# A 3x3 convolution stage on one core: four combinations of kept rows moved behind the last step's first additions, and split by images in the last output half

## The chip, the cores and the metric

The kernel runs on one core of a Trainium2 chip. Its time is the device time of one execution in microseconds (us); lower is better. A core has TensorE (PE: matrix products into PSUM, an accumulator memory of eight banks), VectorE (DVE), ScalarE (ACT), GpSimd (POOL), and DMA queues that are fed from SyncE (SP) and from POOL. Each engine works through its own list of instructions in order; semaphores make one engine wait for another, and an instruction of an engine wait for an earlier one of its own.

## What is computed

For an input `x` of 8 images with 512 channels of 32x32 in float32:

```python
def _L0_conv_ref(x, ...):                 # C = 256, 4 heads of 64, N = 2
    t = cbs(x, cv1_w, cv1_bn, 0)          # cbs: convolution, batch norm, SiLU
    ys = [t[:, :C], t[:, C:]]
    for i in range(N):
        yi = ys[-1]
        z = cbs(yi, m_cv1_w[i], m_cv1_bn[i], 1)      # the 3x3 convolution
        z = bot_attention(z, m_qkv_w[i], m_rw[i], m_rh[i])
        z = silu(bn_eval(conv2d(z, m_cv2_w[i], 0), m_cv2_bn[i]))
        ys.append(yi + z)
    return cbs(concatenate(ys, axis=1), cv2_w, cv2_bn, 0)
x = x + _L0_conv_ref(_gn(x), ...)         # _gn: group norm, 32 groups
```

The change is inside the 3x3 convolution `z = cbs(yi, m_cv1_w[i], ...)`.

## The kernel before

**Passes.** The eight images go through in four passes of two (`p` = 0 to 3, `G = 2` images a pass). In each pass stand a first 3x3 convolution (`n = 0`), projections and attention of either image, a 1x1 convolution `m2`, then the same with a second 3x3 convolution (`n = 1`), then the output convolution `cv2`. The products of `cv1` for the next pass are laid between. So there are eight 3x3 convolutions, each for both images at once. Projections, `cv1` and `cv2` mostly use Strassen's seven products instead of eight.

**The 3x3 convolution** (`conv3x3`, L610). It uses a Winograd form for tiles of 4x4 outputs: the input rows and columns are transformed to six values each (`v_in`, made by DVE before), the weights too (`u`, loaded), PE multiplies, and DVE transforms back. For each of two output halves of 128 channels (`oc`) there are three steps `i`, one for each pair of the six row values; a step has 96 matrix instructions in the profile.

In a step PE first writes the products of four of the six column values into one PSUM tile (`inner_ps`), then those of the other two into a second one (`outer_ps`). Both come from the pool `ps_big`, which has room for three tiles in turn, so a tile is free again for PE once DVE has read the one that stood there three tiles earlier. Then:

- ACT copies one bank of the inner tile to SBUF (`c_m`, L658);
- DVE adds and subtracts the other bank and the copy (`c_t`, L672 and L673; the *additions* below). L673 is the last to read the inner tile. In the last step of the last output half (`parts = groups`) both are split into one for each image;
- L680 (`c_e`) brings in the outer tile, and is the last to read it; L687 to L690 make the two rows `r0`, `r1` (`c_r`);
- steps 0 and 1 keep their sum and difference (`c_k`, L693 and L694): `s_`, `d_` from step 0, `big_s`, `big_d` from step 1;
- at the end of step 1 come **the four combinations of kept rows** (L698 to L701): output rows 1 and 2 of each tile are written from the kept values, and `big_s`, `big_d` are overwritten by what rows 0 and 3 need;
- in step 2, the last one, L703 and L704 (first and last output row) finish `z`, and ACT applies batch norm and SiLU in place (L495), for each image and each half of its rows.

In step 1 of the last output half, POOL also forms the difference `t_z` (`first_sum`, L900) out of the already finished output half 0, for the projection behind (not in pass 0's first convolution).

**The projection behind** (`project_strassen`, L902) starts with image 0: first PE products of output half 0 (`to_qk`, L916), then `to_v` (L922) into a tile of `ps_big`, then L916 on output half 1, which needs the last SiLU of image 0. Pass 0's first convolution is followed by a plain projection (`project_direct`) instead. `q` stands in the SBUF place of the additions' results, and `kr` in that of the kept rows.

**What sets the order.** The Tile framework's scheduler orders every engine's list when the program is built; `with tc.issue_after(x)` forbids it to put what is inside ahead of `x`. ACT keeps one set of function tables; a change from SiLU to Exp or back costs an ACT_TABLE_LOAD.

Of the kernel before, what the change touches and what calls it, by code (L numbers as in the profile page):

```python
# [47 lines left out]
ALU = mybir.AluOpType  # L48
# [13 lines left out]
def kernel(  # L62
# [43 lines left out]
    stt, tt = nc.vector.scalar_tensor_tensor, nc.vector.tensor_tensor  # L106
# [384 lines left out]
    def stages(act, small, ps_big, ps_av, n_pt):  # L491
# [16 lines left out]
        def table_of(func):  # L508

            return nc.scalar.activation(spare, zero, func)  # L510
# [99 lines left out]
        def conv3x3(n, vs, u_of, z, groups=G, summed=None, after=None, between={}):  # L610

            q = TILES * groups
            work = act.tile([P, 2, 2, 4, q], F32, tag="q", name="c3_t")
            keep = act.tile([P, 2, 2, 4 * q], F32, tag="k", name="c3_k")
            turn, t = 0, None
            s_, d_, big_s, big_d = (keep[:, i, j] for i in range(2) for j in range(2))

            def tiles(ap):
                return ap.rearrange("p (t w) -> p t w", w=F)

            for oc in range(NM):
                dst = z[:, oc].rearrange("p g x -> p (g x)").rearrange("p (t r w) -> p r t w", r=4, w=F)
                for i in range(NI):
                    us = u_of(oc, i)
                    m = work[:, turn % 2]
                    turn += 1
                    e_t = act.tile([P, 4 * q], F32, tag="rs", name="c3_e", bufs=4)
                    inner_ps, outer_ps = (
                        ps_big.tile([P, 2, HALF], F32, tag="big", name="c3_ps") for _ in range(2)
                    )  # L630

                    def slots(ps, bank):
                        return ps[:, bank, : 4 * q].rearrange("p (r a q) -> p r a q", r=2, a=2)

                    places = {
                        1: (inner_ps, 0, 0), 2: (inner_ps, 1, 0), 3: (inner_ps, 0, 1), 4: (inner_ps, 1, 1),
                        0: (outer_ps, 0, 0), 5: (outer_ps, 0, 1),
                    }
                    for cps in ((1, 2), (0,)):
                        if (turn, cps[0]) in between:  # L640
                            between[turn, cps[0]](conv_product[0])
                        for row in range(2):
                            for cp in cps:
                                for c in range(2):
                                    ps, bank, at = places[CPS[cp][c]]
                                    to = slots(ps, bank)[:, row, at]
                                    for k in range(NM):
                                        rhs = vs[i, cp][:, c].rearrange(
                                            "p g (r t k s) -> p g r t k s", r=2, t=NT, k=NM
                                        )[:, :, row, :, k]  # L650
                                        for h in range(2):
                                            o = slice(h * HD, (h + 1) * HD)
                                            conv_product[0] = nc.tensor.matmul(  # L653
                                                to[o], us[cp][:, k, row, c, o], rhs,
                                                start=(k == 0), stop=(k == NM - 1),
                                            )
                    m24 = act.tile([P, 2, 2, q], F32, tag="h", name="c3_m", bufs=2)
                    copied = nc.scalar.copy(m24, slots(inner_ps, 1))  # L658
                    if after:
                        with tc.issue_after(copied.ins):  # L660
                            after()
                        after = None
                    r_t = act.tile([P, 8 * q], F32, tag="acc", name="c3_r", bufs=2)
                    final = i == NI - 1
                    parts = groups if final and oc == NM - 1 else 1
                    n_q = q // parts
                    by_part = {"g": parts, "r": 2, "q": n_q}
                    m_t = m.rearrange("p r a q -> p (r a q)")
                    m_parts = m_t.rearrange("p (g r a q) -> p g r a q", a=4, **by_part)
                    for part in range(parts):  # L670
                        qs, m = ts(part, n_q), m_parts[:, part]
                        tt(m[:, :, 0::2], slots(inner_ps, 0)[..., qs], m24[..., qs], ALU.add)  # L672
                        tt(m[:, :, 1::2], slots(inner_ps, 0)[..., qs], m24[..., qs], ALU.subtract)  # L673
                    for part in range(parts):
                        qs, tl, xs_ = ts(part, n_q), ts(part, n_q // NT), ts(part, 4 * n_q)
                        m = m_parts[:, part]
                        e = e_t.rearrange("p (g r a q) -> p g r a q", a=2, **by_part)[:, part]
                        r = r_t.rearrange("p (g r t x s) -> p g r t x s", g=parts, r=2, x=4, s=NT)[:, part]
                        outer = slots(outer_ps, 0).rearrange("p r a q -> p (r a) q")[..., qs]
                        stt(e.rearrange("p r a q -> p (r a) q"), outer, -6.0, m[:, :, 0:2], ALU.mult, ALU.add)  # L680

                        def by_tiles(ap):
                            return ap.rearrange("p r (t s) -> p r t s", s=NT)

                        m0, m1, m2, m3 = (by_tiles(m[:, :, a]) for a in range(4))
                        e0, e1 = (by_tiles(e[:, :, a]) for a in range(2))
                        stt(r[:, :, :, 3], m2, -0.25, e0, ALU.mult, ALU.add)  # L687
                        stt(r[:, :, :, 2], m3, -0.5, m1, ALU.mult, ALU.add)
                        tt(r[:, :, :, 1], m0, m2, ALU.subtract)
                        stt(r[:, :, :, 0], m3, -2.0, e1, ALU.mult, ALU.add)  # L690
                        r0, r1 = (r[:, j].rearrange("p t x s -> p (t x s)") for j in range(2))
                        if i < 2:
                            tt(keep[:, i, 0], r0, r1, ALU.add)  # L693
                            tt(keep[:, i, 1], r0, r1, ALU.subtract)  # L694
                        if i == 1:
                            if oc == NM - 1 and summed is not None:
                                t = first_sum(summed, nc.gpsimd)
                            stt(dst[:, 1], tiles(big_d), -0.5, tiles(d_), ALU.mult, ALU.add)  # L698
                            tt(dst[:, 2], tiles(s_), tiles(big_s), ALU.subtract)
                            stt(big_s, big_s, -0.25, s_, ALU.mult, ALU.add)  # L700
                            stt(big_d, big_d, -2.0, d_, ALU.mult, ALU.add)  # L701
                        if final:
                            stt(dst[:, 0, tl], tiles(r0), -6.0, tiles(big_s[:, xs_]), ALU.mult, ALU.add)  # L703
                            stt(dst[:, 3, tl], tiles(r1), -6.0, tiles(big_d[:, xs_]), ALU.mult, ALU.add)  # L704
                            per = groups // parts
                            for g in range(part * per, (part + 1) * per):
                                for half in range(NH):
                                    z_part = z[:, oc, g, ts(half, HALF)]
                                    last_silu = silu(z_part, z_part, bn_m1[n] + oc)
            if summed is None:  # L710
                with tc.issue_after(last_silu.ins):
                    table_of(AF.Exp)
            return t
# [183 lines left out]
        def first_sum(z, engine=nc.vector):  # L897

            t = act.tile([P, 2, HALF], F32, tag="pt", name="t_z", bufs=n_pt)
            engine.tensor_tensor(t[:, 0], z[:, 0, ts(1, HALF)], z[:, 0, ts(0, HALF)], ALU.subtract)  # L900
            return t
# [836 lines left out]
    with tc.issue_after(made.ins), tc.issue_after(s.silued[0].ins), tc.issue_after(first.ins):  # L1738
        multiplied, read, applied, powered = next(norm)
# [95 lines left out]
    for p in range(NP):  # L1835
# [5 lines left out]
        def u_of(n):  # L1841
            return lambda oc, i: [take(("u", n, oc, i, cp)) for cp in range(3)]
# [337 lines left out]
        if p == 0:  # L2180
            halves = load_halves()
            behind[1] = lambda: make_sw(halves)
            tiles = [act.tile([P, 3 * C], F32, tag=tag, name="qkv_raw") for tag in ("p3", "p4")]
# [198 lines left out]
```

## Time and profile before

| | before |
|---|---|
| median of 3 runs | 2251.07 us (2250.76 to 2251.08) |
| span of the profiled execution, first to last instruction | 2246.8 us |
| PE busy | 2200.9 us (98%) |
| DVE busy | 1728.7 us (77%) |
| ACT busy | 1099.6 us (49%) |
| POOL busy | 224.4 us (10%) |
| granted TensorE clock, mean | 0.999 |

The profile is one execution; its whole time is not given apart from the span, so the span is set beside the median of the runs, 4.27 us above it. Rows of a timeline give the start, the duration, the engine, the line, the operation, output<-inputs and their sizes, and in brackets the idle time of the engine just before and what ended it. The start is from the beginning of the span. An instruction's duration covers its whole way through the engine: the next one often starts before it has ended. Rows of the waits give total time, how often, and the longest. The chain of waits goes back from the last instruction, at each step to what released it.

### The profile page before, as it was taken

The numbers are of one execution on the slowest core, as the hardware profiler recorded it, in microseconds if no ns is written. First come the engines' busy times: TensorE is split into PE (matmuls) and PEld (weight loads), VectorE is DVE, ScalarE is ACT, GpSimd is POOL, SyncE is SP. The second block draws the span as 40 slices with busy tenths as digits, with TensorE's granted clock in tenths as the row PEclk, the third lists the DMA queues.
The fourth block names the chain that finished last, engine by engine and source line by source line (L and its number), as shares of the span: only waits on it lengthen the run. The fifth ranks groups of instructions, "written<-read, shape, count | busy, mean of one in ns | idle before, by whom it ended". The sixth has DMA issues, their size and how long they took to land.

```text
span 2246.8 us, 40264 instructions
## 1 busy us (share of the span) xinstructions
PE 2200.9 (98%) x16346; PEld 1080.6 (48%) x16346; DVE 1728.7 (77%) x2648; ACT 1099.6 (49%) x1332; POOL 224.4 (10%) x417
## 2 busy tenths in 40 slices
PE   7999999999999999999999999999999999999998
PEld 3653437343474444634447343654344734473443
DVE  7988879878678688877857868986794868797652
ACT  7554653644225665456324666455622455335533
POOL 4322210000220000000021000000012000000001
PEclk9999999999999999999999999999999999999999
DMA  9854447321581324511257141532136611350214
GB/s 273 308 163 150 150 151 261 109 78 45 140 275 49 118 81 145 183 58 67 67 159 261 30 169 35 197 116 77 58 76 173 233 39 34 102 198 30 67 50 112
DMA packets 134309, 285.60 MB, mean 127 GB/s; under 512 B 33540, under 2 KB 61184, under 8 KB 133092
## 3 DMA queue, kind: packets, MB, share of 16 engines
q1 hardware_dynamic: 102212, 197.34, 26.7%
q0 software_dynamic: 31904, 85.61, 13.3%
q8 instruction: 131, 2.15, 0.4%
q14 instruction: 62, 0.51, 0.1%
HBM read 214.86 MB, written 68.03 MB: 126 GB/s over the span
## 4 chain that ended last, share of the span: by engine, by line
PE 85%; DVE 11%; issue 1%; ACT 1%; DMA 1%; SPq 0%; POOL 0%; DVEq 0%; ACTq 0%; POOLq 0%
PE av_ps L1071 18%; PE l_ps L1037 18%; PE c L1305 9%; PE c_ps L653 7%; PE c_new L1305 6%; PE p_ps L916 6%; PE ps L523 5%; PE m_ps L1285 5%; PE x_ps L1405 4%; PE p_ps L922 3%; PE s_ps L1089 1%; DVE acc L1057 1%; DVE c_e L680 1%; PE p_ps L886 1%; DVE c_t L673 1%
## 5 line engine op out<-in xcount | busy, mean ns | idle before, releaser
L1041 ACT ACTIVATE pt<-l_ps 128x1024 f32<-128x1024 f32 x512 | 495.5, 1023 | 332.1 <-PE l_ps L1037 218.8
L1057 DVE TENSOR_TENSOR acc<-acc,pt 128x1024 f32<-128x1024 f32 x384 | 469.6, 1223 | 44.6 <-ACT pt L1041 16.2
L1071 PE MATMUL av_ps<-pt,vT 64*64 64x512 f32 x4096 | 484.8, 590 | 5.2 <-DVE z L1079 4.9
L1037 PE MATMUL l_ps<-q,kr 64*64 64x512 f32 x4096 | 486.3, 590 | 3.0 <-ACT pt L1041 1.9
L1071 PEld LDWEIGHTS av_ps<-pt,vT 64*64 64x64 f32 x4096 | 156.3, 133 | 284.8 <-issue 233.5
L1037 PEld LDWEIGHTS l_ps<-q,kr 64*64 64x64 f32 x4096 | 157.5, 133 | 273.2 <-issue 247.0
L653 PE MATMUL c_ps<-v_in,u 128*64 128x128 f32 x4320 | 239.1, 273 | 2.5 <-issue 2.5
L653 PEld LDWEIGHTS c_ps<-v_in,u 128*64 128x64 f32 x4320 | 235.8, 137 | 9.4 <-issue 9.4
L1285 PE MATMUL m_ps<-z,m_sb 128*128 128x512 f32 x256 | 114.1, 593 | 0.0
L658 ACT COPY c_m<-c_ps 128x512 f32<-128x512 f32 x48 | 28.0, 584 | 170.1 <-PE c_ps L653 140.8
L916 PE MATMUL p_ps<-t_z,sq 128*128 128x512 f32 x224 | 107.0, 595 | 0.0
L1079 DVE TENSOR_TENSOR z<-av_ps,z 128x512 f32<-128x512 f32 x64 | 44.1, 689 | 79.1 <-ACT z L1078 79.1
L1055 DVE TENSOR_TENSOR acc<-pt 128x1024 f32<-128x1024 f32 x64 | 78.0, 1219 | 18.0 <-PE s_ps L1089 11.2
L495 ACT ACTIVATE t<-m_ps,bh,sh 128x512 f32<-128x512 f32 x64 | 46.3, 773 | 91.2 <-PE m_ps L1285 91.2
L916 PE MATMUL p_ps<-z,sq 128*128 128x512 f32 x168 | 80.1, 604 | 5.3 <-ACT z L495 5.2
L1355 POOL DMA_DIRECT2D c_out<-in_x_dram x56 | 50.2, 954 | 293.2 <-ACT c_out L495 288.5
L1285 PEld LDWEIGHTS m_ps<-z,m_sb 128*128 128x128 f32 x256 | 47.8, 190 | 56.8 <-issue 52.5
L1147 DVE TENSOR_TENSOR z<-z,rs 128x512 f32<-128x512 f32 x64 | 42.3, 686 | 27.4 <-DMA rs<-r_dram 27.2
L495 ACT ACTIVATE c_out<-cz,bh,sh 128x512 f32<-128x512 f32 x14 | 16.8, 1301 | 89.1 <-DVE cz L1382 89.1
L495 ACT ACTIVATE z<-z,bh,sh 128x512 f32<-128x512 f32 x64 | 47.6, 804 | 25.8 <-DVE z L704 25.2
L1405 PE MATMUL x_ps<-t_x,sw 128*128 128x512 f32 x128 | 55.9, 592 | 0.0
L922 PEld LDWEIGHTS p_ps<-sq,z 128*128 128x128 f32 x336 | 42.7, 191 | 26.6 <-issue 12.7
(313 smaller groups left out, 3143.4 us busy)
## 6 DMA issues: line engine op xcount, KB each, us to landing
u<-u SPq DMA_DIRECT2D x135, 512.0 KB, 4.8
rs<-r_dram SPq DMA_DIRECT2D x126, 128.0 KB, 3.1
sq<-sq SPq DMA_DIRECT2D x42, 384.0 KB, 5.9
x<-in_x_dram SPq DMA_DIRECT2D x28, 512.0 KB, 7.0
r_in<-r SPq DMA_DIRECT2D x28, 512.0 KB, 4.9
y_in<-y SPq DMA_DIRECT2D x28, 512.0 KB, 4.4
c_out<-in_x_dram POOLq DMA_DIRECT2D x56, 256.0 KB, 5.1
out_dram<-c_out POOLq DMA_DIRECT2D x56, 256.0 KB, 3.3
```

Source lines behind the costliest of these rows:

```text
L495: silued[0] = nc.scalar.activation(dst, src, AF.Silu, scale=sh[:, k : k + 1], bias=bh[:, k : k + 1])
L523: last_product[0] = nc.tensor.matmul(ps[:, half, :], w_of(k), rhs_of(k, half), start=(k == begin), stop=(k == end))
L653: conv_product[0] = nc.tensor.matmul(to[o], us[cp][:, k, row, c, o], rhs, start=(k == 0), stop=(k == NM - 1),)
L916: nc.tensor.matmul(ps[:, o, :], w[:, o, :], rhs, start=not onto, stop=True, skip_group_check=onto)
L922: nc.tensor.matmul(v[:, ts(j, P)], rhs[:, ts(j, P)], w[:, 2, :], start=j == 0 and not onto, stop=True, skip_group_check=True,)
L1037: nc.tensor.matmul(ps[kh * HD : (kh + 1) * HD, hd, :], kr[r, c, o : o + HD], q[r, c, ts(half, HALF)], start=True, stop=True,)
L1041: last_exp[0] = exp = nc.scalar.activation(pt, ps, AF.Exp, scale=SCALE)
L1057: ins = nc.vector.tensor_tensor(accs[g], accs[g], pt[i], ALU.add)
L1071: nc.tensor.matmul(avs[g][hd * HD : (hd + 1) * HD, kh, :], vT[r, j, o : o + HD], pt[i][r, hd, :], start=(j == 0), stop=(j == NJ - 1),)
L1285: nc.tensor.matmul(pss[half][:, oc, :], m2_sb[:, n, k, ts(oc, P)], ao[:, k, ts(half, HALF)], start=(k == 0), stop=(k == NM - 1),)
L1305: nc.tensor.matmul(ps[:, o, :], w[:, k, ts(o, P)], rhs[part][:, c], start=(k == 0 and not onto), stop=(k == KB - 1), skip_group_check=onto,)
L1405: nc.tensor.matmul(ps[:, o, :], w[:, c, ts(o, P)], rhs[c], start=(c == 0 and not onto), stop=(c == 1), skip_group_check=onto,)
```

## The change

In the last step (`final`) the additions now remember the last of them (`read`), and the four combinations are issued behind it, for each part of the step. In output half 0 there is one part, so the combinations keep their size and only move from the end of step 1 to behind the additions of step 2. In output half 1 there are two parts, one for each image, so each combination becomes two of half the size, and each image's four stand ahead of that image's L680.

```diff
                     for part in range(parts):
                         qs, m = ts(part, n_q), m_parts[:, part]
                         tt(m[:, :, 0::2], slots(inner_ps, 0)[..., qs], m24[..., qs], ALU.add)
-                        tt(m[:, :, 1::2], slots(inner_ps, 0)[..., qs], m24[..., qs], ALU.subtract)
+                        read = tt(m[:, :, 1::2], slots(inner_ps, 0)[..., qs], m24[..., qs], ALU.subtract)
                     for part in range(parts):
                         qs, tl, xs_ = ts(part, n_q), ts(part, n_q // NT), ts(part, 4 * n_q)
                         m = m_parts[:, part]
+                        if final:
+                            s_p, d_p, big_s_p, big_d_p = (a[:, xs_] for a in (s_, d_, big_s, big_d))
+                            with tc.issue_after(read.ins):
+                                stt(dst[:, 1, tl], tiles(big_d_p), -0.5, tiles(d_p), ALU.mult, ALU.add)
+                                tt(dst[:, 2, tl], tiles(s_p), tiles(big_s_p), ALU.subtract)
+                                stt(big_s_p, big_s_p, -0.25, s_p, ALU.mult, ALU.add)
+                                stt(big_d_p, big_d_p, -2.0, d_p, ALU.mult, ALU.add)
...
                         if i == 1:
                             if oc == NM - 1 and summed is not None:
                                 t = first_sum(summed, nc.gpsimd)
-                            stt(dst[:, 1], tiles(big_d), -0.5, tiles(d_), ALU.mult, ALU.add)
-                            tt(dst[:, 2], tiles(s_), tiles(big_s), ALU.subtract)
-                            stt(big_s, big_s, -0.25, s_, ALU.mult, ALU.add)
-                            stt(big_d, big_d, -2.0, d_, ALU.mult, ALU.add)
```

Lines behind the inserted seven move: what was L680 is now L687, L687 to L690 are L694 to L697, L693 and L694 are L700 and L701, and from L703 on every line is 3 higher. The combinations are now L680 to L683.

**DVE, the end of a convolution** (pass 0, second convolution, output half 1, from the kept sums of step 1 to the outputs of image 0). Before:

```order
L694 TENSOR_TENSOR c_k<-c_r 128x512
L699 TENSOR_TENSOR z<-c_k 128x16x32
L698 SCALAR_TENSOR_TENSOR z<-c_k 128x16x32
L700 SCALAR_TENSOR_TENSOR c_k<-c_k 128x512
L701 SCALAR_TENSOR_TENSOR c_k<-c_k 128x512
L672 TENSOR_TENSOR c_t<-c_ps,c_m 128x4x64
L673 TENSOR_TENSOR c_t<-c_ps,c_m 128x4x64
L672 TENSOR_TENSOR c_t<-c_ps,c_m 128x4x64
L673 TENSOR_TENSOR c_t<-c_ps,c_m 128x4x64
L680 SCALAR_TENSOR_TENSOR c_e<-c_ps,c_t 128x256
```

Now the same place:

```order
L701 TENSOR_TENSOR c_k<-c_r 128x512
L672 TENSOR_TENSOR c_t<-c_ps,c_m 128x4x64
L673 TENSOR_TENSOR c_t<-c_ps,c_m 128x4x64
L672 TENSOR_TENSOR c_t<-c_ps,c_m 128x4x64
L673 TENSOR_TENSOR c_t<-c_ps,c_m 128x4x64
L680 SCALAR_TENSOR_TENSOR z<-c_k 128x8x32
L681 TENSOR_TENSOR z<-c_k 128x8x32
L683 SCALAR_TENSOR_TENSOR c_k<-c_k 128x256
L682 SCALAR_TENSOR_TENSOR c_k<-c_k 128x256
L687 SCALAR_TENSOR_TENSOR c_e<-c_ps,c_t 128x256
```

The additions stand first, and only image 0's half of the combinations is ahead of its L680. L682 overwrites `big_s`, which L681 reads, and L683 overwrites `big_d`, which L680 reads; the list has L683 between L681 and L682. A little later, the first combination of image 1 stands where the second L680 stood, ahead of image 0's outputs:

```order
L697 SCALAR_TENSOR_TENSOR c_r<-c_t,c_e 128x16x8
L680 SCALAR_TENSOR_TENSOR z<-c_k 128x8x32
L706 SCALAR_TENSOR_TENSOR z<-c_r,c_k 128x8x32
L707 SCALAR_TENSOR_TENSOR z<-c_r,c_k 128x8x32
L681 TENSOR_TENSOR z<-c_k 128x8x32
L683 SCALAR_TENSOR_TENSOR c_k<-c_k 128x256
L682 SCALAR_TENSOR_TENSOR c_k<-c_k 128x256
L687 SCALAR_TENSOR_TENSOR c_e<-c_ps,c_t 128x256
```

The rest of image 1's combinations follows image 0's outputs (L706 and L707).

**ACT, at the same place.** The scheduler also moves the SiLUs of image 1 (`z`), here from between image 0's and the copies of the projection to behind the first copy to `q`, which waits for DVE and PE. Before, and then now:

```order
L959 COPY m_z<-p_ps 128x1024
L495 ACTIVATE z<-z,bh,sh 128x512 x4
L961 COPY u_zv<-p_ps 128x512
L962 COPY m_zv<-p_ps 128x512
L968 COPY q<-p_ps 128x512
L973 COPY kr<-p_ps 128x512
L974 COPY q<-p_ps 128x512
L970 COPY vT<-p_ps 128x4x128
L975 COPY vT<-p_ps 128x4x128
```

```order
L962 COPY m_z<-p_ps 128x1024
L495 ACTIVATE z<-z,bh,sh 128x512 x2
L964 COPY u_zv<-p_ps 128x512
L965 COPY m_zv<-p_ps 128x512
L971 COPY q<-p_ps 128x512
L495 ACTIVATE z<-z,bh,sh 128x512 x2
L973 COPY vT<-p_ps 128x4x128
L976 COPY kr<-p_ps 128x512
L977 COPY q<-p_ps 128x512
L978 COPY vT<-p_ps 128x4x128
```

Seven of the eight convolutions, all but pass 0's first, have this order behind them. PE's list changes there too: the `to_v` products of one block now stand between the L916 products of that block and the next, with the same products in all.

**ACT, behind pass 0's first convolution.** Before, the two SiLUs of `y_half` (a result of `cv1`) stood on either side of image 1's SiLUs and of the load of the Exp table; now both stand ahead, and with them two table loads are gone (one here, one ahead of the first exponential). Now:

```order
L495 ACTIVATE z<-z,bh,sh 128x512 x2
L495 ACTIVATE y_half<-ps,bh,sh 128x16x8x4
L429 ACTIVATE u_new<-ypad_67 128x2x128
L430 COPY u_new<-ypad_67 128x2x128
L495 ACTIVATE z<-z,bh,sh 128x512 x2
L510 ACT_TABLE_LOAD
L510 ACTIVATE spare<-zero 128x1
L871 COPY q<-ps 128x1024
```

The lists of POOL and SP do not change.

## The prediction

> **What bounds the kernel now.** I read the page first, then the waits of PE, then the chain of waits and the timelines around the ends of the eight convolutions. The page says whose time it is:
>
> ```profile
> span 2246.8 us, 40264 instructions
> PE 2200.9 (98%) x16346; PEld 1080.6 (48%) x16346; DVE 1728.7 (77%) x2648; ACT 1099.6 (49%) x1332; POOL 224.4 (10%) x417
> ```
>
> PE is idle for 2246.8 - 2200.9 = 45.9 us in all, so a change on DVE can only win what PE waits for. The waits of PE (total us, times, longest) name four groups that the change can reach:
>
> ```profile
> PE p_ps L916 <- ACT z L495: 5.2, 6, 0.9
> PE c_ps L653 <- issue: 2.5, 4, 0.6
> PE p_ps L922 <- DVE c_t L673: 2.5, 4, 0.6
> PE l_ps L1037 <- ACT pt L1041: 1.9, 4, 0.7
> ```
>
> The first three stand at the ends of convolutions. The chain of waits shows how the second convolution of pass 0 ends (start, us, what):
>
> ```profile
> 364.70 0.69 DVE c_e L680
> ...
> 372.31 0.60 DVE c_k L694
> 372.91 0.60 DVE z L699
> ...
> 374.72 0.60 DVE c_k L701
> 375.32 0.34 DVE c_t L672
> ...
> 377.58 0.20 DVE c_r L690
> ...
> 378.45 0.35 DVE z L704
> 378.82 0.82 ACT z L495
> ...
> 379.69 3.70 PE p_ps L916 x8
> ```
>
> From 364.70 on, DVE works without a break and PE follows it: the last SiLU waits for L704, and PE's next product for that SiLU. Of the same end, PE's timeline has two more waits:
>
> ```profile
> 360.09 12.45 PE L653 MATMUL c_ps<-v_in,u 128*64 128x128 f32 x224 [0.63 <-issue]
> ...
> 376.80 1.13 PE L922 MATMUL p_ps<-sq,z 128*128 128x128 f32 x8 [0.63 <-DVE c_t L673]
> ```
>
> Both are waits for a PSUM tile that L673 is last to read: inside the convolution (L653 needs the tile of the last step of output half 0) and behind it. So each of the four second convolutions loses 0.63 + 0.63 + 0.87 = 2.13 us, and the first convolutions of passes 1 and 2 lose 0.87 each (six SiLU waits, 5.2 us).
>
> **The change, the tail of a second convolution.** Before, between L694 and the SiLU stand four combinations of 0.60, four additions of 0.333 (375.32, and the next 0.34 on), L680 of 0.33, four c_r of 0.20, L680 of the other image pair 0.34, L703 0.33 and L704 0.42: 2.41 + 1.33 + 0.33 + 0.80 + 0.34 + 0.33 + 0.42 = 5.96 us; the chain says 378.82 - 372.91 = 5.91. After, the additions come first, and only the first image's combinations are ahead of its outputs, in pieces of 256 elements; one combination of the second image takes the place of the second L680. For the price of a piece I take the operation of that shape, and for an instruction that must wait for the one right before it a pair from pass 0:
>
> ```profile
> 378.37 0.42 DVE L704 SCALAR_TENSOR_TENSOR z<-c_r,c_k 128x256 f32<-128x256 f32 x1
> ...
> 133.27 0.42 DVE L439 SCALAR_TENSOR_TENSOR u_new<-ypad,u_new 128x256 f32<-128x256 f32 x1
> 133.73 0.42 DVE L440 SCALAR_TENSOR_TENSOR u_new<-ypad,u_new 128x256 f32<-128x256 f32 x1
> ```
>
> A 256-element piece lasts 0.42, but starts come 0.333 apart (the c_t of the chain). L440 overwrites what L439 reads and starts 0.46 behind it, 0.12 more; the new order has one other piece between the one that reads big_s and the one that overwrites it, and the same for big_d, so this is not paid. The tail: additions 1.33, combinations 1.33, L680 0.33, c_r 0.80, one piece 0.33, L703 0.33, L704 0.42, together 4.87. Against 5.96 that is 1.09, against the chain's 5.91 1.04; I take 1.06. PE would be ready earlier by both 0.63 waits, which go because L673 reads 2.4 us earlier, but what is late next is the same SiLU, so they win nothing on top: 0.63 + 0.63 + 0.87 becomes one wait of 2.13 - 1.06 = 1.07. **4 x 1.06 = 4.24 us.** Bounds: 0.63 each if every one of the five pieces ahead of the outputs took its whole 0.42 (0.43 more); 2.13 each, all that PE waits there, is out, since DVE's instructions alone fill 4.87.
>
> The Trainium skill ("VectorE: DVE Perf Modes", section "The DRAIN you can't avoid") says that the next Vector operation cannot start before the pipeline has emptied. By that rule each piece costs its whole 0.42 and the sum for this term would be 2.5; the trace disagrees, with starts 0.333 apart at 0.42 each.
>
> **Output half 0, where a cover goes.** The additions need ACT's copy c_m. Before, the four combinations hid it; now DVE waits behind `read` with nothing in between. Where DVE lags, the copy is long done, where it doesn't, not (DVE's L699 is the place where the first addition now stands):
>
> ```profile
> 354.30 0.59 ACT L658 COPY c_m<-c_ps 128x512 f32<-128x512 f32 x1 [4.82 <-PE c_ps L653]
> 356.30 0.69 DVE L699 TENSOR_TENSOR z<-c_k 128x512 f32<-128x512 f32 x1
> ...
> 370.87 0.59 ACT L658 COPY c_m<-c_ps 128x512 f32<-128x512 f32 x1 [4.18 <-issue]
> ...
> 653.81 0.68 DVE L699 TENSOR_TENSOR z<-c_k 128x512 f32<-128x512 f32 x1
> 654.01 0.59 ACT L658 COPY c_m<-c_ps 128x512 f32<-128x512 f32 x1 [4.70 <-PE c_ps L653]
> ```
>
> In second convolutions both copies (354.89, 371.46) end before DVE is there. In the first convolution of pass 1 the copy ends at 654.60: DVE loses 0.80 + 0.03 = 0.83; I take the same for passes 2 and 3, whose steps have the same shapes. Part of it comes back, from POOL:
>
> ```profile
> 663.15 1.79 DVE L687 SCALAR_TENSOR_TENSOR c_r<-c_t,c_e 128x256 f32<-128x256 f32 x1
> ...
> 663.36 1.29 POOL L900 TENSOR_TENSOR t_z<-z 128x512 f32<-128x512 f32 x1
> ...
> 675.05 1.01 ACT L959 COPY m_z<-p_ps 128x1024 f32<-128x1024 f32 x1 [0.70 <-PE p_ps L916]
> ...
> 677.84 3.70 PE L916 MATMUL p_ps<-z,sq 128*128 128x512 f32 x8 [0.87 <-ACT z L495]
> ```
>
> While POOL subtracts, a DVE instruction with two SBUF inputs stands still (1.79 instead of 0.42, 1.37 lost). DVE, 0.83 later, meets it one instruction earlier, at L688, and is released at the same time, so it leaves only L687, 0.33 later than before. The end of this convolution then is 1.06 - 0.33 = 0.73 earlier; ACT's m_z copy (to 676.06) still lets the SiLU go. **2 x 0.73 = 1.46** for passes 1 and 2; between 0.23 each (POOL's work moves with DVE's, and nothing of the 0.83 comes back) and the whole 0.87.
>
> **Pass 3, first convolution.** Here the trace has no wait to win:
>
> ```profile
> 1759.93 0.69 DVE L693 TENSOR_TENSOR c_k<-c_r 128x512 f32<-128x512 f32 x1
> ...
> 1761.06 1.31 POOL L900 TENSOR_TENSOR t_z<-z 128x512 f32<-128x512 f32 x1
> ...
> 1771.15 0.41 DVE L704 SCALAR_TENSOR_TENSOR z<-c_r,c_k 128x256 f32<-128x256 f32 x1
> ...
> 1771.96 2.93 ACT L495 ACTIVATE z<-z,bh,sh 128x512 f32<-128x512 f32 x4
> ...
> 1772.83 3.70 PE L916 MATMUL p_ps<-z,sq 128*128 128x512 f32 x8
> ```
>
> L704 ends at 1771.56, and the SiLU waits 0.40 longer for ACT. POOL's subtraction now meets only additions that read PSUM. With DVE 0.83 later it meets L693 (1760.76 to 1761.45), two SBUF inputs, issued 0.30 before it, as L687 in pass 1 was issued 0.21 before it and stood still. DVE loses another 1.37: 1.06 won in the tail, 0.83 + 1.37 lost, L704 ends 1.14 later, of which the SiLU's 0.40 hides a part, and PE starts 0.74 later. **-0.74**; 0 if POOL gives way.
>
> The Trainium skill ("SBUF — State Buffer", "Who interferes with whom") gives the lock: a Vector instruction with two SBUF inputs and a GpSimd instruction that reads SBUF exclude each other, and the one issued first goes on. L687's row agrees with the lock and not with that order; by the page L693 would go on, and this term would be 0.
>
> **Pass 0, first convolution.** Its last SiLU waits for an earlier ACT instruction, not for DVE, so the tail wins nothing. But the scheduler now puts the second y_half SiLU ahead of the second image's z, and the Exp table is loaded once instead of in turns; the load ahead of the first exponential goes:
>
> ```profile
> 125.25 1.27 ACT L495 ACTIVATE y_half<-ps,bh,sh 128x512 f32<-128x512 f32 x1 [4.74 <-PE ps L523]
> 126.32 3.05 ACT L495 ACTIVATE z<-z,bh,sh 128x512 f32<-128x512 f32 x4
> ...
> 147.40 1.28 ACT L1041 ACT_TABLE_LOAD   x1
> ...
> 149.77 1.09 PE L1037 MATMUL l_ps<-q,kr 64*64 64x512 f32 x8 [0.70 <-ACT pt L1041]
> ```
>
> The exponential starts 1.28 earlier and the 0.70 goes: **0.70**, between 0 and 0.70.
>
> **Sum.** 4.24 + 1.46 - 0.74 + 0.70 = 5.66 us off a span of 2246.8, giving 2241.1. The median 2251.07 is the span and 4.3 around it, which the change doesn't touch: 2245.4. The work behind the convolutions starts from PE, so I let it all move with PE. A measurement of this kernel tells about 0.2% from no change, 4.5 us: the forecast lies 1.2 beyond it.
>
> **The rivals.** *POOL gives way in pass 3's first convolution*: 4.24 + 1.46 + 0.70 = 6.4, so 2244.7; with the whole 0.87 in passes 1 and 2, 6.7 and 2244.4. For it: L693 is twice as long as L687 and under way. Against: L687's row. The Trainium skill's order of issue would give this. Chance 0.29, faster by over 0.2%.
>
> *The pieces pay their whole 0.42.* 0.43 more in each convolution: 4 x 0.63 + 2 x 0.30 + 0.70 - (0.74 + 0.43) = 2.65, so 2248.4, within 0.2%. Against it stand the starts in the chain. The rule of the Trainium skill on the drain would give this. Chance 0.09. *Half is lost again* in attention, where PE would wait for DVE's sums or a transfer instead: 2.8 stay, 2248.3, within 0.2%; against it, those stages begin with PE's own products. Chance 0.17.
>
> *ACT's queue turns the sign.* In the new order ACT's copy of q waits for DVE, and behind it stand the second image's SiLUs and then the copies to vT, which free the PSUM tile of PE's s3 product:
>
> ```profile
> 386.24 0.58 ACT L975 COPY vT<-p_ps 128x512 f32<-128x512 f32 x1 [1.25 <-PE p_ps L922]
> ...
> 387.79 1.88 PE L916 MATMUL p_ps<-t_z,sq 128*128 128x512 f32 x4
> ```
>
> Behind the first image's outputs (372.91 + 4.87 = 377.78) come three pieces, L680, four c_r, t_z and the two outputs: 1.00 + 0.33 + 0.80 + 0.60 + 0.75, so 381.3. The two SiLUs run to 382.8, four copies of about 0.5 to 384.9, and PE needs the tile at 387.79 - 1.06 = 386.73: 1.8 of slack. It decides only once the last copy is over 1.8 late; to end 4.5 above before, the seven convolutions with this order must each lose (5.7 + 4.5) / 7 = 1.5, so be 3.3 late: 2255.6. Chance 0.05. *The change does nothing for PE* is out: its additions free the tile by order alone.
>
> **How the numbers follow.** The forecast has the remaining 0.40, and 0.07 of it lies under 4.5, since a few tenths at each of seven ends could be missing. Faster 0.33 + 0.29 = 0.62; within 0.2% 0.07 + 0.09 + 0.17 = 0.33; slower 0.05. The range goes from 2243.9, the first rival's 2244.4 with 0.07 more at each of seven ends, to 2249.2, the two cases near 2248.4 with 0.1 less at each; the slower case is left out.
>
> **What would show it.** Right: no PE wait for c_t L673 and no 0.63 inside second convolutions; one SiLU wait there about 1.1 long; starts 0.333 apart in all eight combinations of the last output half; DVE idle 0.8 ahead of the additions of output half 0 in first convolutions of passes 1 to 3; a stretched DVE instruction beside POOL's t_z in pass 3; no table load ahead of the first exponential. The forecast is wrong if the SiLU waits of second convolutions come out far from 1.1, if pass 3's first convolution has no PE wait, or if new PE waits stand in the projections or attention.

## The result, and the profile after

| | before | after |
|---|---|---|
| median | 2251.0 us (2249.31 to 2251.88, 12 runs) | 2245.92 us (2244.81 to 2247.26, 12 runs) |
| ratio to before, 95% interval | | 0.9977, 0.9969 to 0.9985 |
| span of the profiled execution | 2246.8 us | 2244.4 us |
| mean granted TensorE clock | 0.999 | 0.998 |

The kernel became 5.1 us faster; 2245.4 was forecast. The profiled spans are only 2.4 apart, and this has to be settled before terms are read from them. PE's timeline of before, at the first product of the first convolution and at the last product of all (start, us, engine, line, what, and in brackets the wait before it):

```profile
75.05 2.19 PE L653 MATMUL c_ps<-v_in,u_new 128*64 128x128 f32 x36 [1.76 <-DVE v_in L607]
...
2237.45 0.19 PE L2283 MATMUL g_ps<-ones,good 128*1 128x1 f32 x2
```

The same two places after:

```profile
75.78 1.42 PE L653 MATMUL c_ps<-v_in,u_new 128*64 128x128 f32 x22 [2.54 <-DVE v_in L607]
...
2232.94 0.19 PE L2286 MATMUL g_ps<-ones,good 128*1 128x1 f32 x2
```

Between the two stand 2162.40 us before and 2157.16 after: 5.24 less, as the medians say. The other 2.8 us of the profiled execution went to its start, ahead of the changed code, and to what follows the last product. So below "gain" is always taken between starts of the same product, counted from the first product of the first convolution.

The page and the waits of PE after show which waits went:

```profile
PE 2199.2 (98%) x16346; PEld 1080.9 (48%) x16346; DVE 1729.1 (77%) x2680; ACT 1097.5 (49%) x1330; POOL 224.6 (10%) x417
```

```profile
PE p_ps L919 <- ACT z L495: 7.3, 6, 1.5
...
PE l_ps L1040 <- ACT pt L1044: 1.2, 3, 0.5
```

The rows "c_ps <- issue" and "p_ps <- DVE c_t", 2.5 each before, are gone, and `l_ps` waits 0.7 less. The SiLU wait grew from 5.2 in all to 7.3, its longest from 0.9 to 1.5. Of the end of pass 0's second convolution, DVE's timeline:

```profile
372.02 0.68 DVE L701 TENSOR_TENSOR c_k<-c_r 128x512 f32<-128x512 f32 x1
372.63 0.42 DVE L672 TENSOR_TENSOR c_t<-c_ps,c_m 128x256 f32<-128x256 f32 x1
...
373.95 0.42 DVE L680 SCALAR_TENSOR_TENSOR z<-c_k 128x256 f32<-128x256 f32 x1
374.28 0.42 DVE L681 TENSOR_TENSOR z<-c_k 128x256 f32<-128x256 f32 x1
...
376.43 0.42 DVE L680 SCALAR_TENSOR_TENSOR z<-c_k 128x256 f32<-128x256 f32 x1
...
377.10 0.42 DVE L707 SCALAR_TENSOR_TENSOR z<-c_r,c_k 128x256 f32<-128x256 f32 x1
```

The pieces start 0.33 apart at 0.42 each, one piece of the second image (376.43) stands ahead of image 0's outputs, and from L672 to the end of L707 it takes 377.52 - 372.63 = 4.89, where 4.87 was worked out. ACT and PE behind it:

```profile
377.56 1.52 ACT L495 ACTIVATE z<-z,bh,sh 128x512 f32<-128x512 f32 x2 [1.32 <-DVE z L707]
```

```profile
357.74 13.81 PE L653 MATMUL c_ps<-v_in,u 128*64 128x128 f32 x248
...
378.42 1.98 PE L919 MATMUL p_ps<-z,sq 128*128 128x512 f32 x4 [1.46 <-ACT z L495]
380.24 1.05 PE L925 MATMUL p_ps<-sq,z 128*128 128x128 f32 x8
381.13 1.88 PE L919 MATMUL p_ps<-z,sq 128*128 128x512 f32 x4
383.02 1.16 PE L925 MATMUL p_ps<-sq,z 128*128 128x128 f32 x8
```

One unbroken row of 248 products in place of two with 0.63 between, and one wait of 1.46. New is that PE turns from L919 to L925 and back behind the first four products; before, the eight of them (L916 then) stood together.

### The profile page after: what moved, and what is told of

The parts are those of the page before. It is cut to its first block, busy times and chain, and to the rows that moved or that the text cites. A ratio compares the mean times of both kernels' runs of the same rounds, so it can differ in the third digit from the quotient of the medians.

```text
span 2244.4 us, 40286 instructions
## 1 busy us (share of the span) xinstructions
PE 2199.2 (98%) x16346; PEld 1080.9 (48%) x16346; DVE 1729.1 (77%) x2680; ACT 1097.5 (49%) x1330; POOL 224.6 (10%) x417
## 4 chain that ended last, share of the span: by engine, by line
PE 85%; DVE 11%; issue 1%; ACT 1%; DMA 1%; SPq 0%; POOL 0%; DVEq 0%; ACTq 0%; POOLq 0%
PE av_ps L1074 18%; PE l_ps L1040 17%; PE c L1308 9%; PE c_ps L653 8%; PE c_new L1308 6%; PE p_ps L919 6%; PE ps L523 5%; PE m_ps L1288 5%; PE x_ps L1408 4%; PE p_ps L925 3%; DVE acc L1060 2%; PE s_ps L1092 1%; PE p_ps L889 1%; DVE c_e L687 1%; DVE c_r L695 1%
## 5 line engine op out<-in xcount | busy, mean ns | idle before, releaser
L919 PE MATMUL p_ps<-t_z,sq 128*128 128x512 f32 x224 | 105.9, 595 | 0.0
L919 PE MATMUL p_ps<-z,sq 128*128 128x512 f32 x168 | 81.3, 604 | 7.3 <-ACT z L495 7.3
L919 PEld LDWEIGHTS p_ps<-t_z,sq 128*128 128x128 f32 x224 | 39.5, 191 | 36.5 <-issue 34.4
```

Of the source, the lines that this page charges most:

```text
L919: nc.tensor.matmul(ps[:, o, :], w[:, o, :], rhs, start=not onto, stop=True, skip_group_check=onto)
```

## The experiments

My theory (A): PE resumes behind a convolution when DVE's chain to image 0's last SiLU ends, so only what leaves that chain counts. Rivals: (B) the early release of PSUM tiles is the gain; (C) what stands still beside POOL's `t_z` is covered by other work. The gains of each kernel at the eight ends, in us (p1n0 is pass 1's first convolution; the last columns are the whole trace, which is one execution and in which a few tenths stand between the ends, and the difference of the medians on the same chip):

| kernel | p0n0 | p0n1 | p1n0 | p1n1 | p2n0 | p2n1 | p3n0 | p3n1 | whole trace | by the medians |
|---|---|---|---|---|---|---|---|---|---|---|
| the change | 0.93 | 0.97 | 0.45 | 0.96 | -0.04 | 0.85 | -0.05 | 0.96 | 5.24 | 5.08 |
| first half only | -0.32 | 0.03 | -0.63 | 0.01 | -0.16 | 0.01 | -1.62 | 0.03 | -2.30 | -1.12 |
| last half only | 0.93 | 1.00 | 0.96 | 0.63 | 0.97 | 0.98 | -0.05 | 0.98 | 7.03 | 6.84 |
| not split | 0.44 | -1.65 | -0.29 | -1.67 | -0.64 | -1.69 | -1.11 | -1.66 | -7.69 | -6.62 |
| not split, last half only | 0.44 | 0 | -0.12 | 0 | -0.07 | -0.03 | -1.05 | 0 | -0.84 | -0.02 |
| second convolutions only | 0 | 0.96 | -0.12 | 0.96 | 0.20 | 0.73 | 0 | 0.97 | 4.26 | 4.21 |
| pass 0's first only | 0.93 | 0.02 | 0.17 | 0.02 | 0.20 | 0.02 | 0 | 0.04 | 1.82 | 1.51 |
| the change, `t_z` on DVE | 0.93 | 1.22 | 0.96 | 1.22 | 0.98 | 0.37 | -0.05 | 1.21 | 6.94 | 6.94 |
| last half only, `t_z` on DVE | 0.93 | 1.23 | 0.96 | 1.23 | 0.98 | 1.21 | -0.05 | 1.21 | 8.24 | 7.98 |

Three cells are low because PE waits once in the first half of that convolution, away from the changed place: 0.63 in "last half only" (a wait of 0.30), 0.73 in "second convolutions only" (0.18) and 0.37 in "the change, `t_z` on DVE" (0.80). Why was not traced.

**One half of the change at a time.** In output half 0 alone, the combinations stand behind the additions; in the last half the old order stays:

```diff
-                        if final:
+                        if final and (oc < NM - 1):
...
                             if oc == NM - 1 and summed is not None:
                                 t = first_sum(summed, nc.gpsimd)
+                            if not (oc < NM - 1):
+                                stt(dst[:, 1], tiles(big_d), -0.5, tiles(d_), ALU.mult, ALU.add)
...
```

The second kernel has `oc == NM - 1` in both places.

> The four combinations stand behind the additions in output half 0 only; in output half 1 they stay at the end of step 1, unsplit, as before the change. Theory A (the tail of DVE's work ahead of image 0's last SiLU sets the gain): no second convolution gains, since DVE has as much to do ahead of that SiLU; the 0.63 wait for L653 goes, and the waits behind it grow by the same. First convolutions lose, since DVE waits 0.7 to 0.8 us for ACT's copy in output half 0: 0.3 to 0.8 each in passes 1 and 2, about 0.4 in pass 3. In all 1 to 2 us slower than before, 2252 to 2253. Theory B (the gain is PSUM given back to PE earlier): the four 0.63 waits, worth 0.89 each in the trace after, are won: 3.6 us faster, about 2247.4.

> The reverse of the run before: combinations split and behind the additions in output half 1 only; output half 0 as before the change. Theory A: second convolutions gain the same 0.95 each as with the whole change (3.8), with the 0.63 wait for L653 back and the SiLU wait shorter by that; first convolutions of passes 1 and 2 no longer wait for ACT's copy in output half 0 and win 0.7 each; the first exponential's table load is gone, 0.88. In all 6.0 us faster than before, about 2245.0, and 0.8 faster than the whole change. Theory B: the 4 x 0.89 of the first wait is lost again: only 1.7 us faster than before, about 2249.3.

First half only: 2251.74 us, 1.0007 (0.9998 to 1.0017). The time by itself can't be told from before, and lies just under the 2252 to 2253 expected by A; B's 2247.4 is far off. The wait inside the convolution is gone, and comes back behind it. PE's timeline of the same end as above:

```profile
354.77 17.08 PE L653 MATMUL c_ps<-v_in,u 128*64 128x128 f32 x308
...
376.88 1.13 PE L930 MATMUL p_ps<-sq,z 128*128 128x128 f32 x8 [1.40 <-DVE c_t L673]
```

0.63 became 1.40, and all four second convolutions gain nothing. That is A, and B falls. In the first convolutions it costs 0.32, 0.63, 0.16 and 1.62. The last is far over the 0.4 expected: there a DVE operation beside POOL's `t_z` lasted 1.58 in place of 0.42.

Last half only: 2243.78 us, 0.9970 (0.9959 to 0.9981), faster than A's 2245.0. DVE at the place in pass 1's first convolution where the whole change lets it wait for `c_m`, and PE at the end of pass 0's second and pass 1's first:

```profile
653.26 0.68 DVE L709 SCALAR_TENSOR_TENSOR c_k<-c_k 128x512 f32<-128x512 f32 x1
653.86 0.68 DVE L672 TENSOR_TENSOR c_t<-c_ps,c_m 128x512 f32<-128x512 f32 x1
```

```profile
358.71 12.45 PE L653 MATMUL c_ps<-v_in,u 128*64 128x128 f32 x224 [0.62 <-issue]
...
377.24 1.98 PE L924 MATMUL p_ps<-z,sq 128*128 128x512 f32 x4 [0.67 <-ACT z L495]
...
674.47 1.98 PE L924 MATMUL p_ps<-z,sq 128*128 128x512 f32 x4
```

The old 0.62 inside the convolution is back, the last wait is 0.79 shorter than the 1.46 of the whole change, and the end gains the same 1.0. The early release of half 0's tile is worth nothing there, while in the first convolutions the old order there saves DVE's idle time: 0.96 and 0.97 in place of 0.45 and -0.04.

**Without the split.** Both halves late, the combinations as four operations of 512 elements:

```diff
-                        if final:
-                            s_p, d_p, big_s_p, big_d_p = (a[:, xs_] for a in (s_, d_, big_s, big_d))
+                        if final and part == 0:
                             with tc.issue_after(read.ins):
-                                stt(dst[:, 1, tl], tiles(big_d_p), -0.5, tiles(d_p), ALU.mult, ALU.add)
+                                stt(dst[:, 1], tiles(big_d), -0.5, tiles(d_), ALU.mult, ALU.add)
...
```

> The whole change without the split by images: in output half 1 too, the four combinations keep their full size and stand behind the additions, ahead of image 0's outputs. Both PSUM waits go as with the whole change. Theory A: DVE's work ahead of image 0's last SiLU is as long as before, so second convolutions gain nothing (0 to 0.3 each), first convolutions lose 0.3 to 0.8 each, and the table load gives 0.88: between 0.5 faster and 1.5 slower than before, 2250.5 to 2252.5, with SiLU waits of about 2.1. Theory B: both waits are won, 4 x (0.89 + 0.73) and 0.88: 7 us faster, about 2244.

2257.24 us, 1.0030 (1.0020 to 1.0039): 6.6 slower, which no theory had. Both PSUM waits are gone, and yet PE resumes behind the second convolutions no more than 0.03 earlier than before, which speaks against B once more. DVE's tail is not longer: from the first addition to the end of L706 it is 378.63 - 372.68 = 5.95, where 5.96 was summed for before. PE waits once, and then its products take longer. DVE, the windows and PE of the same end:

```profile
372.68 0.42 DVE L672 TENSOR_TENSOR c_t<-c_ps,c_m 128x256 f32<-128x256 f32 x1
...
378.22 0.41 DVE L706 SCALAR_TENSOR_TENSOR z<-c_r,c_k 128x256 f32<-128x256 f32 x1
```

```profile
376.00:379.00 3.00, 1.02 (x10) 0.83 (x8) 3.00 (x12) 0.62 (x2) 0.00 (x0) 1.00 0.25 58
379.50:381.50 2.00, 1.97 (x3) 0.94 (x4) 1.95 (x5) 2.00 (x4) 0.00 (x0) 0.51 0.24 83
381.50:383.20 1.70, 1.70 (x4) 0.74 (x3) 0.68 (x2) 1.04 (x2) 0.00 (x0) 0.57 0.00 0
```

```profile
379.53 5.38 PE L918 MATMUL p_ps<-z,sq 128*128 128x512 f32 x8 [2.51 <-ACT z L495]
```

In the windows the column behind POOL's is the granted clock: 1.00 up to the wait, 0.51 and 0.57 behind it, where the 3.70 us of eight products become 5.38, 1.68 lost. In all four second convolutions a wait of 2.50 or 2.51 stands before it, and all four lose 1.65 to 1.69. Of this kernel's ten executions, nine had a mean granted clock of 0.995 or 0.996 and took 2256.05 to 2258.48; one had 0.998, as before the change, and took 2252.55, close to the upper end of A's 2250.5 to 2252.5. In pass 0's first convolution both `y_half` SiLUs stand ahead of image 0's `z` in this order, PE waits 0.73 there in place of 0.21, and of the 0.93 some 0.49 is lost. To tell the clock from the unsplit order itself, the next kernel keeps the order but not the long wait: unsplit as above, in the last half alone (`if final and oc == NM - 1 and part == 0`, output half 0 as before).

> The four combinations behind the additions in the last output half alone, and not split by images (512 elements each, all ahead of image 0's outputs); output half 0 has the order of before. The kernel that did this in both halves was 6.6 us slower than before; its PE waited once for 2.51 us at the end of each second convolution, and granted the clock 0.51 to 0.57 for the 3.4 us behind that. Theory A with the clock (the tail is as long as before, 5.97 us, and the loss is the half clock behind one wait of 2.51): output half 0 keeps its 0.63 of waiting, the last wait is 0.63 + 0.87 = 1.5 to 1.7 long, no half clock follows, and with the pass 0 table load gone the time is 2249.5, between 2249.0 and 2251.0. Rival (the loss belongs to the unsplit order itself, as ACT's SiLUs of image 1 then stand ahead of the m_zv copy): 4 x 1.6 stay lost, 2255 to 2257.

2250.24 us against 2250.22, 0.9999 (0.9990 to 1.0008). The windows and PE at the same end:

```profile
379.50:381.50 2.00, 1.72 (x4) 0.87 (x5) 1.92 (x5) 2.00 (x4) 0.00 (x0) 1.00 0.71 246
381.50:383.20 1.70, 1.70 (x5) 0.76 (x4) 0.93 (x2) 1.70 (x4) 0.00 (x0) 1.00 0.00 0
```

```profile
360.18 12.45 PE L653 MATMUL c_ps<-v_in,u 128*64 128x128 f32 x224 [0.63 <-issue]
...
379.79 3.70 PE L923 MATMUL p_ps<-z,sq 128*128 128x512 f32 x8 [1.74 <-ACT z L495]
```

The idle time is divided into 0.63 and 1.74, the clock stays at 1.00, and the second convolutions are even with before, with the same list of ACT at this end as in the kernel before it. So moving the combinations without splitting them is worth nothing, as A says, and the loss in the second convolutions was the half clock behind one long wait. The split is what takes work out of the chain.

**Where it counts.** The change in the second convolutions alone (`n == 1`), and in pass 0's first convolution alone (`n == 0 and summed is None`):

> The change in the second convolutions of the four passes alone; the first ones have the order of before. Theory A (the second convolutions gain by the shorter tail ahead of image 0's last SiLU, 0.84 to 0.96 each in the changed kernel's trace, 3.7 together; the pass 0 table load and the 0.5 of the first convolutions stay out): 2250.7 - 3.7 = 2247.0 us. Theory B (the early release of both PSUM tiles, 1.26 each, is what a second convolution wins): 2245.7. A theory by which the gain comes from the first convolutions and the table load: 2249.5 or more.

> The whole change in the first convolution of pass 0 alone; the other seven convolutions as before. If the table load ahead of the first exponential is what PE waits for there, that load is gone, the wait of the logits' product for the exponential (0.70) is gone, and everything behind it is 0.7 to 0.9 us earlier: about 2250.1. If the wait only moves, the load is gone and the products behind it stand where they stood: 2251.0.

Second convolutions only: 2246.01 us, 0.9984 (0.9975 to 0.9993), 4.2 faster. The time lies between A's 2247.0 and B's 2245.7 and can't tell them apart; the trace can: one wait of 1.46 as in the whole change, 0.96, 0.96, 0.73 and 0.97 won, 3.6 of the 4.26. The table load ahead of the first exponential is still there, in ACT's timeline:

```profile
147.09 1.28 ACT L1049 ACT_TABLE_LOAD   x1
148.38 3.77 ACT L1049 ACTIVATE pt<-l_ps 128x1024 f32<-128x1024 f32 x4
```

Pass 0's first only: 2249.11 us, 0.9994 (0.9984 to 1.0003), unclear by itself. Its trace has the load gone and the product that waited 0.70 for that exponential 0.9 earlier.

**POOL's subtraction.** The changed kernel with `t_z` of the last half on DVE, `t = first_sum(summed)` in place of `t = first_sum(summed, nc.gpsimd)`, and the same for the kernel with the last half only:

> The changed kernel, with the subtraction t_z of the last output half on DVE (one 128x512 operation, 0.60 from start to start) instead of POOL. Changed kernel beside it: 2245.9 us. Theory A (DVE's chain sets the ends, and the instruction that stands still beside POOL's t_z is on that chain): taken away are 0.74 in each of the four second convolutions (L695 1.16 instead of 0.42), 1.07 in the first one of pass 1 (1.48), 1.56 in that of pass 2 (1.98) and nothing in pass 3; paid are 0.60 in each of the seven. 4 x 0.14 + 0.47 + 0.96 = 2.0 faster, less up to 0.6 for pass 3: 2243.9 to 2244.5. Theory C (the stretched instruction is covered by other work and costs nothing): seven times 0.60 more, 2250.1.

> The kernel that makes the change only in the last output half (2243.8 us), with t_z of the last half on DVE instead of POOL. Theory A: taken away are 0.74 in each second convolution (L695 1.15), 1.14 in the first one of pass 1 (L700 1.82), 0.74 in that of pass 2 (L695 1.15), 0.80 in that of pass 3 (L696 1.21), where ACT holds the SiLU anyway; paid are 0.60 in each. 4 x 0.14 + 0.54 + 0.14 = 1.2 faster: 2242.5 us. Theory C (the stretch costs nothing): 4.2 slower, 2248.0.

2243.28 us, 0.9969 (0.9957 to 0.9982), and 2242.24 us, 0.9966 (0.9954 to 0.9978). A held and C fell: DVE has seven operations more and the ends come earlier, the first kernel 0.6 below the range that A gave it. In second convolutions 0.25 was won, not 0.14; DVE's timeline of the first of the two kernels shows why:

```profile
365.37 0.42 DVE L697 SCALAR_TENSOR_TENSOR c_r<-c_t,c_e 128x256 f32<-128x256 f32 x1
365.70 0.69 DVE L903 TENSOR_TENSOR t_z<-z 128x512 f32<-128x512 f32 x1
366.30 0.69 DVE L700 TENSOR_TENSOR c_k<-c_r 128x512 f32<-128x512 f32 x1
```

L903 stands where L700 had to wait 0.12 for L697 right before it, so the 0.12 went too. The second is the fastest kernel of the study, by its median. Its interval overlaps that of the change and those of its neighbours, so that it beats them rests on the traces: 8.24 against 5.24.

## Why the prediction was right, and where it was not

The time, the sign and the main mechanism came out as forecast: 5.24 in the trace against a sum of 5.66. The terms were less right than the sum, and that the sum came so close is in part luck: 0.50 and 1.05 too much in the second convolutions and in the first ones of passes 1 and 2, 0.69 and 0.23 too little in pass 3 and pass 0. Two of the prediction's own signs of being wrong came: the SiLU waits are 1.45 and 1.46, not about 1.1, and pass 3's first convolution has no PE wait. The 4.3 us that it put around the span isn't a fixed amount either: after, the median stands 1.5 above the profiled span.

**Second convolutions: 4.24 forecast, 3.74 measured.** The chain on DVE is as summed (4.89 against 4.87), and PE resumes 1.06 or 1.07 earlier at three of the four ends, where 1.06 was forecast. Three things around it were mis-sized. The step that took the three waits as 0.63 + 0.63 + 0.87 = 2.13 was too low: the unsplit kernel, whose tail is as long as before, has them as one wait of 2.51. The change takes 5.95 - 4.89 = 1.06 off it, so 1.45 is left over, not 1.07. That alone moves no time, since PE resumes with the SiLU all the same. What does is the order of PE's list behind it, which I had not costed. From the product that the SiLU releases to the last products of the projection (`pv_ps`), PE took 392.12 - 379.69 = 12.43 before and takes 390.95 - 378.42 = 12.53 now, so 0.10 is given back at each such end. In pass 2 another 0.11 is lost to a short wait in the first half of the convolution.

**First convolutions of passes 1 and 2: 1.46 forecast, 0.41 measured.** The idle time in front of the additions was right: the row lists 0.73, and DVE is 0.82 later against PE behind it, where 0.83 was summed: L695, 662.47 now, stood at 662.82 before (as L688), 0.35 earlier, while PE is earlier there by its gain so far less the later start, 0.93 + 0.97 - 0.73 = 1.17. Two steps failed, that POOL gives part of it back in both passes, and that the end costs nothing more (the 0.10 of PE's order). DVE's and POOL's timelines after, pass 1:

```profile
653.46 0.69 DVE L672 TENSOR_TENSOR c_t<-c_ps,c_m 128x512 f32<-128x512 f32 x1 [0.73 <-ACT c_m L658]
...
662.36 1.29 POOL L903 TENSOR_TENSOR t_z<-z 128x512 f32<-128x512 f32 x1
662.47 1.48 DVE L695 SCALAR_TENSOR_TENSOR c_r<-c_t 128x256 f32<-128x256 f32 x1
```

and pass 2:

```profile
1209.12 1.98 DVE L695 SCALAR_TENSOR_TENSOR c_r<-c_t 128x256 f32<-128x256 f32 x1
...
1209.52 1.28 POOL L903 TENSOR_TENSOR t_z<-z 128x512 f32<-128x512 f32 x1
```

I had held POOL's subtraction at its old time, and pass 2 to be like pass 1. Against PE's products it came 0.17 later in pass 1, 0.67 in pass 2 and 0.77 in pass 3. In POOL's list it stands right behind the issue of a store of results (`out_dram`, L1359), ahead of which POOL is idle for 1.9 to 3.3 us; what moved that was not traced. In pass 1 it gives 1.37 - 1.06 = 0.31 back, close to the 0.33 of the forecast. In pass 2 an operation of the same size stood still before too:

```profile
1211.43 1.80 DVE L687 SCALAR_TENSOR_TENSOR c_r<-c_t,c_e 128x256 f32<-128x256 f32 x1
```

1.80 before and 1.98 after, so 0.18 is lost there, not 0.33 won. 1.06 - 0.82 + 0.31 - 0.10 = 0.45 and 1.06 - 0.82 - 0.18 - 0.10 = -0.04, as in the table. The two kernels with `t_z` on DVE gain 0.96 and 0.98 in both.

**Pass 3's first convolution: -0.74 forecast, -0.05 measured.** The forecast collision did not come. DVE, POOL, ACT and PE after:

```profile
1757.76 0.69 DVE L701 TENSOR_TENSOR c_k<-c_r 128x512 f32<-128x512 f32 x1
1758.22 1.35 POOL L903 TENSOR_TENSOR t_z<-z 128x512 f32<-128x512 f32 x1
...
1767.44 1.01 ACT L962 COPY m_z<-p_ps 128x1024 f32<-128x1024 f32 x1 [0.70 <-PE p_ps L919]
1768.35 1.52 ACT L495 ACTIVATE z<-z,bh,sh 128x512 f32<-128x512 f32 x2
...
1769.22 1.98 PE L919 MATMUL p_ps<-z,sq 128*128 128x512 f32 x4
```

POOL came 0.77 later against PE, nearly as much as DVE, and met L701 (L694 before) 0.46 after that had started; L701 kept its 0.69, as L694 had before, 0.51 ahead of POOL. For this end the rival "POOL gives way" came out, but not by its mechanism, and its 2244.7 did not follow, since passes 1 and 2 brought less. In the kernel that is unsplit in the last half alone, the same operation (L700 there) started 0.24 ahead of POOL and stood still, and that end lost 1.05. Its DVE and POOL at this place:

```profile
1760.88 2.09 DVE L700 TENSOR_TENSOR c_k<-c_r 128x512 f32<-128x512 f32 x1
...
1761.12 1.28 POOL L907 TENSOR_TENSOR t_z<-z 128x512 f32<-128x512 f32 x1
```

So the price of the step was real (2.09 in place of 0.69, where 1.37 was to be lost), and POOL's timing spared the changed kernel. In the changed kernel DVE is ready early, but the SiLU stands behind ACT's `m_z` copy and PE waits for neither. By the order of issue that the Trainium skill gives ("SBUF — State Buffer", "Who interferes with whom") L701 goes on, and does; L695 in pass 2 was issued 0.40 ahead of POOL by the recorded starts and by that rule should have gone on too, and stood still for 1.98.

**Pass 0: 0.70 forecast, 0.93 measured.** ACT after:

```profile
128.42 1.25 ACT L495 ACTIVATE y_half<-ps,bh,sh 128x512 f32<-128x512 f32 x1
130.07 1.52 ACT L495 ACTIVATE z<-z,bh,sh 128x512 f32<-128x512 f32 x2
131.59 1.28 ACT L510 ACT_TABLE_LOAD   x1
148.15 3.77 ACT L1044 ACTIVATE pt<-l_ps 128x1024 f32<-128x1024 f32 x4
```

One load, 16 us ahead of its use. The wait listed as 0.70 was worth 0.9.

3.74 + 0.41 - 0.05 + 0.93 = 5.03; the other 0.21 stands at one place, two products of `m2` behind pass 1's second convolution, is there in most of the other kernels too, and was not traced to a cause. The slower rival, ACT's copies to `vT`, had the slack it was given: no wait of PE for them stands in the list after. The rivals in which the pieces pay their whole 0.42, or half is lost in attention, are out by the rows above. The section on the drain in the Trainium skill ("VectorE: DVE Perf Modes", "The DRAIN you can't avoid"), which the prediction took as a rule for every operation, itself says that one which is not held starts earlier; the starts 0.33 apart agree with that.

## What to carry to other kernels

A wait that is listed is worth its time only if nothing on the same chain stands behind it: here both PSUM waits could go without gain, and what paid was to take the second image's work out of the chain ahead of the first image's outputs. Move such work only in the stage where its consumer waits; in the other stage the same move uncovered a copy that it had hidden. And look at where the idle time ends up: pieces of idle time that are joined into one can cost more than their sum, here through the half clock that followed 2.5 us of it.

## What the runs showed of the hardware

- In the profiled execution of the unsplit kernel, four of four waits of PE of 2.50 or 2.51 us had some 1.68 us of time lost in the products behind them, at a granted clock of 0.51 to 0.57; none was lost behind ten waits of 1.08 to 1.75 in the unsplit kernels' convolution ends, nor behind the 1.45 and 1.46 of the changed kernel. 1.68 lost at half speed is 3.4 us of half clock. The Trainium skill ("TensorE: Matmul & The Clock Gate", section "What's actually happening") gives a window of 3413 ns, with which that length agrees, and half clock after at least one idle window of about 3.4 us; here 2.5 us of idle time were enough. It doesn't come each time: one of the ten executions had a mean clock of 0.998. Between 1.75 and 2.50 nothing was tried at these ends. At the start of the first convolution half clock followed waits of 2.00, 2.22 and 2.42 us and did not follow 2.37, 2.54 and 3.48, so the length of the wait alone doesn't decide.
- DVE operations with two SBUF inputs, issued 0.21, 0.24 and 0.40 us ahead of the recorded start of POOL's subtraction, stood still until POOL was done; those issued 0.46 and 0.51 ahead did not.
- The idle times that the profile lists were lower than what they were worth: 0.63 + 0.63 + 0.87 joined were 2.51, and the wait of 0.70 was worth 0.9.
